# Turning attention's weights by DMA and VectorE instead of TensorE, with the second use of a pair two pairs later

## The chip, the cores and the metric

One core of a Trainium2 chip runs the whole program. The engines work side by side, each through its own instructions in order: TensorE (PE in the profile; PEld are its weight loads), VectorE (DVE), ScalarE (ACT), GpSimd (POOL) and SyncE (SP), which here only issues DMAs. The metric is device time in microseconds of one execution, as the median of several runs; the profile is of one execution.

## What is computed

The input is 2 images of 128 channels x 64 x 64. Layer 0 is a neighbourhood attention block per image. Layer 1 works on the 4096 tokens of each image: a full self-attention in which queries, keys and values are the same normalised tokens, and then a long-convolution mixer. The part that matters here:

```python
def _L1_attn_ref(q):
    scale = 1.0 / np.sqrt(HIDDEN_SIZE).astype(np.float32)
    sim = jnp.einsum('blh,bmh->blm', q, q) * scale
    diag = jnp.eye(L, dtype=bool)
    sim = jnp.where(diag[None, :, :], jnp.float32(-1000000000.0), sim)
    attn = jax.nn.softmax(sim, axis=-1)
    return jnp.einsum('blm,bmh->blh', attn, q)
...
t = _to_tokens(x)
t = t + _L1_attn_ref(_ln_t(t))
t = t + _L1_ffn_ref(_ln_t(t), ...)
```

All data are float32. `sim` is symmetric, so `exp(sim)` of a block of queries against a block of keys, turned, is the block of the keys against the queries. No maximum is subtracted, so the two halves need no rescaling.

## The kernel before

Stage 0 (to about 346 us) is layer 0, in an order written out by hand. Then come the attention of batch 0 (346 to about 790 us), the attention of batch 1 (to about 1266 us), and the convolution (the rest, from L1392 on). This change is in the attentions (lines 897 to 998).

The 4096 tokens of a batch are 8 chunks of 512. `cm[b]` holds them with channels on partitions (128 x 4096), `tok[b]` with tokens on partitions (32 tiles of 128 x 128). A pair (a, c) is a chunk a of queries against a chunk c >= a of keys: 28 pairs with a != c and 8 diagonal ones per batch, in the order of `pairs` (L910).

- `weights` (L913) makes one quarter k of a pair: a score matmul of 128 queries x 512 keys into a PSUM bank (L918), and ScalarE's exponential into an SBUF tile `e` (L926), which also sums the rows into `part`, the parts of the softmax denominators. On a diagonal pair only the columns from `lo` on are computed; VectorE adds a large negative number on the diagonal (L924), and the rest is filled from the quarters before by transposes (L932) and VectorE (L933).
- For a != c the four `e` are used twice. The first use (L983) multiplies `tok` of chunk a with each `e` and sums in the bank `other`: the output of chunk c. After four quarters VectorE adds it to `xa` (L995, or L997 for a = 0).
- The second use needs the weights turned. `turned` (L938) does this for 128 keys m: four TensorE transposes of 128x128 into a bank (L942), then one VectorE instruction that copies the bank to `et` and sums its rows into `part` (L945). `onto` (L952) multiplies `tok` of chunk c with `et` and sums in the bank `own`, the output of chunk a, over all c. When it is complete, VectorE adds it to `xa` (L960, L962) and `fill` is told.
- The loop (L969 to L998) makes the quarters of the following pair while it uses those of this one. The turned quarters wait in the list `late` and are used one by one behind the next products.
- After each quarter `fill()` does one step of other work: the rest of layer 0 (`drain`), the filter tables (`filters`, L1195; POOL writes `fb`, SP stores `gs` in L1222), the tokens of batch 1, and for each finished chunk `after` (L1003): layer norm, a transform on TensorE, `ub` on VectorE (L1039), and sixteen stores to `us` on SP's queue (L1043, L1048). In batch 1 it also loads and mixes the convolution's weights (`mixed`, L1166, with the loads `st` in L1171, two buffers).

Nothing in the attentions is in a hand-written order: a scheduler of the language places each engine's instructions from the order in which the program makes them, the dependences and its own estimates. Waits are on semaphores. All DMAs that SP issues go round eight completion counters: a DMA waits until the one eight before it has finished.

Of the kernel before, what the change touches and what calls it, by code (L numbers as in the profile page):

```python
# [8 lines left out]
F32 = mybir.dt.float32  # L9
AF = mybir.ActivationFunctionType  # L10
ALU = mybir.AluOpType
# [90 lines left out]
def kernel(  # L102
# [767 lines left out]
    with ap_:  # L870
        tp = ap_.enter_context(tc.tile_pool(name="l1_t", bufs=1, side="right"))
        ep = ap_.enter_context(tc.tile_pool(name="l1_e", bufs=8, side="right"))
        sp = ap_.enter_context(tc.tile_pool(name="l1_s", bufs=2, side="right"))
        ps_o = ap_.enter_context(tc.tile_pool(name="l1_ps_o", bufs=1, space=PSUM))
        ps_m = ap_.enter_context(tc.tile_pool(name="l1_ps_m", bufs=6, space=PSUM))
# [13 lines left out]
        one = tp.tile([P, 512], F32, name="one")  # L889
        nc.gpsimd.memset(one, 1.0)  # L890
# [6 lines left out]
        def attention(b, fill):  # L897
# [15 lines left out]
            def weights(a, c, k, left=()):  # L913
# [3 lines left out]
                ps = bank()  # L917
                nc.tensor.matmul(  # L918
                    ps[:, lo:], lhsT=cm[b][:, n * P : (n + 1) * P],
                    rhs=cm[b][:, CHUNKS[c] * 512 + lo : (CHUNKS[c] + 1) * 512], start=True, stop=True,  # L920
                )
                if a == c:
                    ks = slice(k * P, (k + 1) * P)
                    nc.vector.tensor_tensor(ps[:, ks], ps[:, ks], ndiag, ALU.add)  # L924
                e = ep.tile([P, 512], F32, tag="e", name="e")
# [3 lines left out]
                if lo:  # L929
                    pt = bank()  # L930
                    for j in range(k):
                        nc.tensor.transpose(pt[:, j * P : (j + 1) * P], left[j][:, lo : lo + P], ident)  # L932
                    nc.vector.tensor_tensor_reduce(  # L933
                        e[:, 0:lo], pt[:, 0:lo], one[:, 0:lo], 1.0, 0.0, ALU.mult, ALU.add, part[:, n, 8:9]
                    )
                return e

            def turned(a, c, m, es):  # L938

                pt = bank()  # L940
                for k in range(4):
                    nc.tensor.transpose(pt[:, k * P : (k + 1) * P], es[k][:, m * P : (m + 1) * P], ident)  # L942
                et = ep.tile([P, 512], F32, tag="et", name="et", bufs=4)
                n = 4 * CHUNKS[c] + m
                nc.vector.tensor_tensor_reduce(  # L945
                    et, pt, one, 1.0, 0.0, ALU.mult, ALU.add, part[:, n, a : a + 1]
                )
                return et

            own = None  # L950

            def onto(a, n, e, first, last):  # L952
                nonlocal own
                if first:
                    own = ps_o.tile([P, 512], F32, tag="own", name="own")
                nc.tensor.matmul(own, lhsT=tok[b][:, n, :], rhs=e, start=first, stop=last)  # L956
                if last:
                    xs = xa[b][:, chunk(a)]
                    if a:
                        nc.vector.tensor_tensor(xs, own, xs, ALU.add)  # L960
                    else:
                        nc.vector.tensor_copy(xs, own)  # L962
                    fill(CHUNKS[a], part)

            late = []
            es = []
            for k in range(4):
                es.append(weights(0, 0, k, es))
            for i, (a, c) in enumerate(pairs):  # L969
                following = pairs[i + 1] if i + 1 < len(pairs) else None  # L970
                coming = []
                if a != c:
                    other = ps_o.tile([P, 512], F32, tag="other", name="other")
                for k in range(0, 4, 2):
                    for j in (k, k + 1):
                        if following:
                            coming.append(weights(*following, j, coming))
                        if a == c:
                            while late:
                                onto(*late.pop(0))  # L980
                            onto(a, 4 * CHUNKS[a] + j, es[j], j == 0, a == 7 and j == 3)
# [740 lines left out]
```

## Time and profile before

| what | value |
|---|---|
| median of 3 runs | 2070.92 us (2066.39 to 2071.28) |
| the profiled execution: its own time, its span | 2070.7 us, 2068.7 us |
| TensorE busy over the span | 1997.5 us (97%) |
| VectorE, ScalarE, GpSimd busy | 997.7 (48%), 733.5 (35%), 472.9 us (23%) |
| granted TensorE clock, mean | 0.989 |
| data moved by DMA | 112.82 MB, 55 GB/s over the span |
| the chain that ended last | TensorE 80%, VectorE 7%, DMA 4%, GpSimd 4% |

The costliest groups of the attentions (line, engine, operation, tiles, shape, count, then busy us in all, mean ns of one, and the idle time just before them with what ended it):

```profile
L926 ACT ACTIVATE e<-bank 128x512 f32<-128x512 f32 (+3 forms) x288 | 161.6, 561 | 519.6 <-PE bank L918 396.5
L918 PE MATMUL bank<-cm 128*128 128x512 f32 (+3 forms) x576 | 277.4, 564 | 1.4 <-DVE y L664 1.4
L956 PE MATMUL own<-et,tok 128*128 128x512 f32 x448 | 230.2, 600 | 8.4 <-DVE part L945 8.1
L983 PE MATMUL other<-e,tok 128*128 128x512 f32 x448 | 229.9, 595 | 4.9 <-DVE xa L995 4.9
L945 DVE CUSTOM_DVE_ANT_0 et<-bank,one 128x512 f32<-128x512 f32 x224 | 146.1, 687 | 128.6 <-PE bank L942 128.4
L942 PE MATMUL bank<-ident,e 128*128 128x128 f32 x896 | 117.1, 274 | 0.0
```

Each float32 matmul is two instructions (448 for 224 products). Their durations overlap, so the mean is longer than what one adds to TensorE's time. ScalarE and VectorE stand idle before their instructions because they wait for TensorE; TensorE waits for next to nothing.

### The profile page before, as it was taken

The numbers are of one execution on the slowest core, as the hardware profiler recorded it, in microseconds if no ns is written. First come the engines' busy times: TensorE is split into PE (matmuls) and PEld (weight loads), VectorE is DVE, ScalarE is ACT, GpSimd is POOL, SyncE is SP. The second block draws the span as 40 slices with busy tenths as digits, with TensorE's granted clock in tenths as the row PEclk, the third lists the DMA queues.
The fourth block names the chain that finished last, engine by engine and source line by source line (L and its number), as shares of the span: only waits on it lengthen the run. The fifth ranks groups of instructions, "written<-read, shape, count | busy, mean of one in ns | idle before, by whom it ended". The sixth has DMA issues, their size and how long they took to land.

```text
span 2068.7 us, 52809 instructions
## 1 busy us (share of the span) xinstructions
PE 1997.5 (97%) x21368; PEld 1436.1 (69%) x21368; DVE 997.7 (48%) x3458; ACT 733.5 (35%) x1974; POOL 472.9 (23%) x781
## 2 busy tenths in 40 slices
PE   6899998999999999999999999999999999999998
PEld 4677775554555554554455554799999899999987
DVE  5899996444544445335733446333333333333332
ACT  3789885322322323212222322222222222222222
POOL 4466887215000000000000000022222121222211
PEclk8999999999999999999999999999999999999999
DMA  4222223003000001004200002222222123222211
GB/s 152 62 61 62 61 60 53 13 21 107 2 25 26 26 26 52 26 0 117 83 26 26 26 26 77 76 67 67 67 67 61 47 58 101 66 67 67 67 45 42
DMA packets 239506, 112.82 MB, mean 55 GB/s; under 512 B 118287, under 2 KB 237215, under 8 KB 238752
## 3 DMA queue, kind: packets, MB, share of 16 engines
q1 hardware_dynamic: 238338, 105.95, 18.9%
q8 instruction: 169, 2.77, 0.6%
q0 software_dynamic: 576, 2.10, 0.3%
q10 hardware_dynamic: 350, 1.41, 0.2%
q14 instruction: 73, 0.60, 0.1%
HBM read 74.78 MB, written 34.63 MB: 53 GB/s over the span
## 4 chain that ended last, share of the span: by engine, by line
PE 80%; DVE 7%; DMA 4%; POOL 4%; ACT 2%; SPq 2%; issue 1%; DVEq 0%; POOLq 0%; ACTq 0%
PE acc L1450 27%; PE own L956 11%; PE bank L918 9%; PE other L983 8%; PE pc L1431 7%; PE bank L942 4%; PE bank L343 2%; PE bank L201 1%; PE bank L1058 1%; PE bank L553 1%; DMA st<-in_m_minus_dram 1%; DMA st<-in_m_plus_dram 1%; ACT p L540 1%; PE bank L1101 1%; PE pc L1489 1%
## 5 line engine op out<-in xcount | busy, mean ns | idle before, releaser
L1436 DVE COPY y<-pc 128x512 f32<-128x512 f32 x320 | 206.2, 686 | 351.4 <-PE pc L1431 351.2
L926 ACT ACTIVATE e<-bank 128x512 f32<-128x512 f32 (+3 forms) x288 | 161.6, 561 | 519.6 <-PE bank L918 396.5
L1450 PE MATMUL acc<-y,mpl 32*128 32x256 f32 x5120 | 324.4, 380 | 0.8 <-DVE af L1460 0.8
L1450 PE MATMUL acc<-y,mmi 32*128 32x256 f32 x5120 | 316.7, 375 | 0.0
L1436 ACT COPY y<-pc 128x512 f32<-128x512 f32 x320 | 171.9, 589 | 400.9 <-PE pc L1431 396.1
L1450 PEld LDWEIGHTS acc<-y,mpl 32*128 32x128 f32 x5120 | 290.0, 186 | 8.2 <-DVE af L1460 1.8
L1450 PEld LDWEIGHTS acc<-y,mmi 32*128 32x128 f32 x5120 | 291.4, 185 | 3.8
L918 PE MATMUL bank<-cm 128*128 128x512 f32 (+3 forms) x576 | 277.4, 564 | 1.4 <-DVE y L664 1.4
L956 PE MATMUL own<-et,tok 128*128 128x512 f32 x448 | 230.2, 600 | 8.4 <-DVE part L945 8.1
L983 PE MATMUL other<-e,tok 128*128 128x512 f32 x448 | 229.9, 595 | 4.9 <-DVE xa L995 4.9
L1431 PE MATMUL pc<-ct,ut 32*128 32x256 f32 x2560 | 215.6, 382 | 5.6 <-DMA ut<-us 3.7
L945 DVE CUSTOM_DVE_ANT_0 et<-bank,one 128x512 f32<-128x512 f32 x224 | 146.1, 687 | 128.6 <-PE bank L942 128.4
L1461 POOL TENSOR_TENSOR af<-af 128x512 f32<-128x512 f32 x39 | 49.7, 1275 | 593.8 <-DVE af L1460 528.1
L173 POOL TENSOR_TENSOR ln_rs<-ln_rs,mhalf 128x4 f32<-128x4 f32 x24 | 24.2, 1009 | 703.6 <-DVE ln_rs L172 703.5
L1431 PEld LDWEIGHTS pc<-ct,ut 32*128 32x128 f32 x2560 | 175.7, 189 | 12.0 <-DMA ut<-us 4.5
L956 PEld LDWEIGHTS own<-et,tok 128*128 128x128 f32 x448 | 82.9, 190 | 121.8 <-issue 60.8
L983 PEld LDWEIGHTS other<-e,tok 128*128 128x128 f32 x448 | 81.7, 190 | 95.0 <-issue 86.9
L942 PEld LDWEIGHTS bank<-ident,e 128*128 128x128 f32 x896 | 103.0, 141 | 46.1 <-issue 39.4
L918 PEld LDWEIGHTS bank<-cm 128*128 128x128 f32 x576 | 94.5, 191 | 54.2 <-issue 38.9
L540 ACT ACTIVATE p<-p,mn 128x196 f32<-128x196 f32 x256 | 114.4, 449 | 13.7 <-DVE mn L530 13.0
L942 PE MATMUL bank<-ident,e 128*128 128x128 f32 x896 | 117.1, 274 | 0.0
L1039 DVE TENSOR_TENSOR ub<-bank,uo 128x256 f32<-128x256 f32 (+1 forms) x192 | 59.5, 373 | 71.1 <-ACT uo L1036 70.2
(258 smaller groups left out, 2530.8 us busy)
## 6 DMA issues: line engine op xcount, KB each, us to landing
ut<-us SPq DMA_DIRECT2D x160, 128.0 KB
us<-ub SPq DMA_DIRECT2D x128, 128.0 KB
ct<-gs SPq DMA_DIRECT2D x320, 40.0 KB
vw<-vd SPq DMA_DIRECT2D x256, 49.0 KB
ct<-gs SPq DMA_DIRECT2D x320, 32.0 KB
vd<-v SPq DMA_DIRECT2D x128, 32.0 KB
st<-in_m_plus_dram SPq DMA_DIRECT2D x16, 256.0 KB
us<-ub SPq DMA_DIRECT2D x128, 32.0 KB
```

Source lines behind the costliest of these rows:

```text
L540: nc.scalar.activation(p, p, AF.Exp, bias=t[name + "mn"][:, h : h + 1], scale=-1.0, accum_out=t["den"][:, u, h : h + 1],)
L918: nc.tensor.matmul(ps[:, lo:], lhsT=cm[b][:, n * P : (n + 1) * P], rhs=cm[b][:, CHUNKS[c] * 512 + lo : (CHUNKS[c] + 1) * 512], start=True, ...
L926: nc.scalar.activation(e[:, lo:], ps[:, lo:], AF.Exp, bias=0.0, scale=ASCALE, accum_out=part[:, n, c : c + 1])
L942: nc.tensor.transpose(pt[:, k * P : (k + 1) * P], es[k][:, m * P : (m + 1) * P], ident)
L945: nc.vector.tensor_tensor_reduce(et, pt, one, 1.0, 0.0, ALU.mult, ALU.add, part[:, n, a : a + 1])
L956: nc.tensor.matmul(own, lhsT=tok[b][:, n, :], rhs=e, start=first, stop=last)
L983: nc.tensor.matmul(other, lhsT=tok[b][:, 4 * CHUNKS[a] + j, :], rhs=es[j], start=(j == 0), stop=(j == 3))
L1039: nc.vector.tensor_tensor(ub[:, sgn, 0:n], pu[s][:, 0:n], half[:, 0:n], op)
L1431: nc.tensor.matmul(pcs[j].rearrange("p (g o c) -> p o g c", g=4, o=2)[:, :, at], lhsT=ut[rows_, par, :], rhs=cv_[rows_], start=True, stop= ...
L1436: (nc.scalar.copy if j % 2 else nc.vector.tensor_copy)(y[:, :, :, 4 * kl + j, :], pcs[j].rearrange("p (g x k) -> p k g x", g=4, k=KF))
L1450: nc.tensor.matmul(acc[j][:, 0:256], lhsT=(mmi if l else mpl)[rows_, k, :], rhs=y[rows_, k, 2 * l : 2 * l + 2].rearrange("p s n x -> p (s ...
L1461: eng.tensor_tensor(af[:, 0:2], af[:, 0:2], af[:, 2:4], ALU.add)
```

## The change

For pairs with a != c, the weights are turned without TensorE. A 128x512 quarter consists of 32x32 blocks; the turned matrix is the blocks moved to their mirrored places, and each block turned in itself.

- The four quarters of a pair lie in one tile of 128 x 2048. The score matmul reads the keys in the order (q, t, j) instead of (t, q, j), with key = 128 t + 32 q + j, so that what must go to one quarter of the partitions is contiguous.
- `moved` issues 16 DMAs on SP's queue. Each copies 32 partitions x 512 numbers from a quarter of the partitions of `e` to another (or the same) quarter of `et`.
- `turned` is now two VectorE transposes of 128x1024, which turn each 32x32 block in place, and one VectorE reduction over 2048 columns into `part` for four key tiles.
- The second use reads `et` in blocks of 32 columns and writes `own` in blocks of 32. It stands in the program four quarters after the transposes' place, which is itself four quarters after the DMAs: one pair (its first use) lies between the DMAs and the transposes, and the second use comes with the pair after that, two products after each of its first quarters. Two `own` banks are in use for this, and five banks instead of six for the rest.
- `other` comes out in the order (q, t, j) and is put back into (t, q, j) by the VectorE instruction that adds it to `xa`.
- On the diagonal pairs, the VectorE instruction that copied and summed at once becomes a copy and a reduction. The tile `one` and its fill go away.
- To make room, the filters' tables `ph` and `fsum` lie in `cm[1]`, which is empty then.

```diff
-        ep = ap_.enter_context(tc.tile_pool(name="l1_e", bufs=8, side="right"))
+        ep = ap_.enter_context(tc.tile_pool(name="l1_e", bufs=2, side="right"))
-        ps_m = ap_.enter_context(tc.tile_pool(name="l1_ps_m", bufs=6, space=PSUM))
+        ps_m = ap_.enter_context(tc.tile_pool(name="l1_ps_m", bufs=5, space=PSUM))
...
+                if k == 0:
+                    halves.append(ep.tile([P, 2048], F32, tag="e", name="e"))
+                eh = halves[0]
+                keys = cm[b][:, chunk(c)]
+                if a != c:
+                    nc.tensor.matmul(
+                        ps.rearrange("p (q t j) -> p q t j", q=4, t=4), lhsT=cm[b][:, n * P : (n + 1) * P],
+                        rhs=keys.rearrange("p (t q j) -> p q t j", t=4, q=4), start=True, stop=True,
+                    )
+                    e = eh.rearrange("p (q k r) -> p k q r", q=4, k=4)[:, k]
+                    nc.scalar.activation(
+                        e, ps.rearrange("p (q r) -> p q r", q=4), AF.Exp, bias=0.0, scale=ASCALE,
+                        accum_out=part[:, n, c : c + 1],
+                    )
+                    return e
...
-                    nc.vector.tensor_tensor_reduce(
-                        e[:, 0:lo], pt[:, 0:lo], one[:, 0:lo], 1.0, 0.0, ALU.mult, ALU.add, part[:, n, 8:9]
-                    )
+                    nc.vector.tensor_copy(e[:, 0:lo], pt[:, 0:lo])
+                    nc.vector.tensor_reduce(part[:, n, 8:9], e[:, 0:lo], AX.X, ALU.add)
...
-            def turned(a, c, m, es):
-
-                pt = bank()
-                for k in range(4):
-                    nc.tensor.transpose(pt[:, k * P : (k + 1) * P], es[k][:, m * P : (m + 1) * P], ident)
-                et = ep.tile([P, 512], F32, tag="et", name="et", bufs=4)
-                n = 4 * CHUNKS[c] + m
-                nc.vector.tensor_tensor_reduce(
-                    et, pt, one, 1.0, 0.0, ALU.mult, ALU.add, part[:, n, a : a + 1]
+            def moved(eh):
+
+                et = ep.tile([P, 4, 512], F32, tag="et", name="et", bufs=2)
+                for q in range(4):
+                    for to in range(4):
+                        nc.sync.dma_start(
+                            out=et[32 * to : 32 * to + 32, q], in_=eh[32 * q : 32 * q + 32, to * 512 : (to + 1) * 512]
+                        )
+                return et
+
+            def turned(et, a, c):
+
+                for q in (0, 2):
+                    flat = et[:, q : q + 2].rearrange("p q r -> p (q r)")
+                    nc.vector.transpose(flat, flat)
+                n0 = 4 * CHUNKS[c]
+                nc.vector.tensor_reduce(
+                    part[:, n0 : n0 + 4, a], et.rearrange("p q (k t i) -> p t (q k) i", k=4, t=4), AX.XY, ALU.add
                 )
...
+            def pair_onto(own, a, c, et, t):
+                onto(
+                    own, 4 * CHUNKS[c] + t, own.rearrange("p (k q i) -> p q k i", k=4, q=4),
+                    et.rearrange("p q (k t i) -> p t q k i", k=4, t=4)[:, t], False, c == 7 and t == 3,
+                )
+                if (c, t) == (7, 3):
+                    complete(a, own)
...
+                e = weights(a, c, k, left, halves)
+                if a != c and k == 3:
+                    et = moved(halves[0])
+                    turns.append((step + 4, et, a, c))
+                    late.extend((step + 5, a, c, et, t) for t in range(4))
+                return e
+
+            def pass_on(n):
+
+                while turns and turns[0][0] <= step:
+                    turned(*turns.pop(0)[1:])
+                while n and late and late[0][0] <= step:
+                    _, a, c, et, t = late.pop(0)
+                    pair_onto(owns[a], a, c, et, t)
+                    n -= 1
...
+                else:
+                    owns[a] = ps_o.tile([P, 512], F32, tag="own", name="own", bufs=2)
+                for j in range(4):
+                    if following:
+                        coming.append(coming_of(*following, j, coming, halves))
+                    n = 4 * CHUNKS[a] + j
+                    if a == c:
+                        onto(owns[a], n, owns[a], es[j], j == 0, a == 7 and j == 3)
+                    else:
+                        nc.tensor.matmul(
+                            other.rearrange("p (q r) -> p q r", q=4), lhsT=tok[b][:, n, :], rhs=es[j],
+                            start=(j == 0), stop=(j == 3),
+                        )
+                    pass_on(2)
+                    fill()
+                    step += 1
```

## The prediction

> **What bounds the kernel now.** I read first the busy time by window, for the two attentions (346 to 790 us is batch 0, 790 to 1266 batch 1), then the list of what TensorE waited for there, then its timeline over one pair of chunks.
>
> ```profile
> core 0: us, PE busy (x) PEld busy (x) DVE busy (x) ACT busy (x) POOL busy (x), PEclk, DMA share, GB/s
> 346.00:790.00 444.00, 436.87 (x1701) 230.13 (x1705) 204.15 (x750) 129.71 (x366) 73.61 (x83) 1.00 0.13 33
> 790.00:1266.00 476.00, 464.22 (x1755) 237.65 (x1749) 225.58 (x743) 120.98 (x357) 9.72 (x11) 1.00 0.14 42
> ```
>
> TensorE is busy for 901 of 920 us at full granted clock. VectorE is busy 47%, the DMA engines 14%: there is room to hand work to them. Some 19 us of TensorE waits are all that exists:
>
> ```profile
> PE own L956 <- DVE part L945: 8.1, 9, 1.6
> PE other L983 <- DVE xa L995: 4.9, 3, 2.5
> ```
>
> So time leaves only with TensorE work, and every new wait of TensorE is paid in full. The timeline of TensorE (start, duration) shows what a pair costs:
>
> ```profile
> 905.50 1.04 PE L942 MATMUL bank<-ident,e 128*128 128x128 f32 x8
> 906.38 1.02 PE L918 MATMUL bank<-cm 128*128 128x512 f32 x2
> 907.24 1.02 PE L983 MATMUL other<-e,tok 128*128 128x512 f32 x2
> 908.09 1.02 PE L956 MATMUL own<-et,tok 128*128 128x512 f32 x2
> ...
> 911.53 1.04 PE L942 MATMUL bank<-ident,e 128*128 128x128 f32 x8
> ```
>
> Starts count here, since durations overlap: a 512-wide float32 product (two instructions) takes 907.24 − 906.38 = 0.86 us, eight transposes 906.38 − 905.50 = 0.88 us. Half a pair is 911.53 − 905.50 = 6.03 us, which is 6 × 0.86 + 0.88. A pair is 12.06 us, of which 1.76 are transposes.
>
> **Removed.** All 896 transposes of L942, 112 groups of eight: 112 × 0.88 = 98.6 us. They lie on the path, since nothing is faster than TensorE there. This is the whole gain; the sum starts from the profiled execution's own 2070.7 us (span 2068.7, 2.0 around it), within 0.2 us of the median of the runs.
>
> **Kept on TensorE, in another shape.** Scores, `other` and the second use `own` keep count and width but read or write in runs of 32 elements. L1431 writes PSUM in permuted pieces at 382 ns, L1450 writes plainly at 380 for the same 256 columns: nothing. For the reads, the bound is the dearest row of the same 128x512 shape, L343 at 658 against 600 ns of L918: 0 to 58 ns on 56 × 12 = 672 products, 0 to 39 us. I take 0, because the nearest row is the permuted one.
>
> **VectorE.** Gone are four reductions with copy per pair, 4 × (0.687 + 0.083) = 3.08 us. New are two 32x32 transpositions of 128x1024 and one reduction of 2048.
>
> ```profile
> L1436 DVE COPY y<-pc 128x512 f32<-128x512 f32 x320 | 206.2, 686 | 351.4 <-PE pc L1431 351.2
> L1460 DVE COPY af<-acc 128x256 f32<-128x256 f32 x80 | 30.4, 420 | 97.8 <-PE acc L1450 95.1 <-ACT af L1460 2.7
> L1461 POOL TENSOR_TENSOR af<-af 128x512 f32<-128x512 f32 x39 | 49.7, 1275 | 593.8 <-DVE af L1460 528.1
> ```
>
> From the two copies: (686 − 420) / 256 = 1.04 ns a column and 154 ns fixed; 1024 columns 1.22 us, 2048 columns 2.28 us. No row is a transposition. Its bounds are 0.96 us (twice the fastest 512-wide VectorE row, L1174 at 481) and 2.55 us (twice GpSimd's 1.275). I take 1.22, the engine's own rate. VectorE then gives 4.72 us per pair instead of 3.08, 56 × 1.64 = 92 us more, some 60% busy in the attentions (430 + 92 of 863 us); that is hidden beside TensorE as long as nothing TensorE needs stands behind it. What does: in the built order of the changed program the usual row on VectorE is first transposition, eviction of `other` (0.69 us), second transposition, reduction. The eviction is ready at the end of a pair, so the second transposition ends 0.8 + 1.22 = 2.02 us into the next pair, where TensorE has a score and an `other` product, 1.72 us, ahead of the second use. Late by 0.3 us: 56 × 0.3 = 17 us. With 0.96 it would be 2, with 2.55 it would be 56 × 1.63 = 91. The 48 diagonal rests (L933) become a copy and a reduction; a copy is no longer than what it replaces and the reduction (0.3 to 0.55 us) is wanted only by the later denominator: 0, at most 5.
>
> The Trainium skill, page "VectorE: DVE Perf Modes", section "The three transpose paths", speaks against the edit: it lists 390 ns for TensorE and 311 ns for VectorE's blocks at 128x128 in bf16, and its rules give the full transposition to TensorE. Eight times 311 would be an estimate of 2.5 us per 128x1024, and the sum 2085 us; no row here shows it, while the copies' slope is 1.04 ns a column.
>
> **The moves.** 56 × 16 = 896 DMAs of 32 partitions x 2 KB (64 KB) are added on SP's queue, 1 MB a pair.
>
> ```profile
> 0.82 1.82 SPq L135 DMA_DIRECT2D xa<-in_x_dram  x4
> 40.28 17.21 SPq L504 DMA_DIRECT2D vw<-vd  x22
> 567.76 4.96 SPq L1043 DMA_DIRECT2D us<-ub  x8
> 574.84 4.51 SPq L1048 DMA_DIRECT2D us<-ub  x8
> ```
>
> SP hands out a DMA every 1.82 / 4 = 0.455 us where each row is one run in one partition (as the moves are), every 17.21 / 22 = 0.78 where partition is an inner dimension. I take 0.455: 7.3 us a pair. From issue to the last completion count, the trace's records have 1.9 us (median of us<-ub, 128 KB) to 2.9 us (st, 256 KB); I take 2.1. Packets: 1 KB takes 46 ns and 4 KB 159 in the records, so some 85 for 2 KB, 512 × 0.085 / 16 = 2.7 us a pair of the sixteen engines. Not a limit.
>
> Is it in time? From the end of a pair's last score to its second use TensorE has an `other` (0.86), four scores and four `other` (6.9), four uses of the pair before (3.4) and a score (0.86): 12.0 us, and the other work between. That is 920 less 56 × 12.06, less 16 × 6.25 (a diagonal, by its products), less 19 idle, over 72 pairs: 1.8. So 13.8 us, and a pair lasts 10.3 + 1.8 = 12.1. Needed: exponential and handover 0.9, 15 issues 6.8, landing 2.1, second transposition 1.3: 11.1. Slack 2.7 us.
>
> SP's other work now queues with the moves, and VectorE's transposition behind them, and TensorE behind that. The stores of `us` (4.96 + 4.51 us a chunk, 16 chunks) hold SP for 4.7 of a pair's 12.1 us, so they meet the moves about four times in ten, with a mean delay of half that, 2.4 us, mostly inside the slack: I take 10 us, bounds 0 and 16 × (9.5 − 2.7) = 109. The 32 loads `st` in batch 1 (L1171) make SP wait 44 us in all for a buffer; before nobody stood behind them, now about five pairs of moves do. I take a third, 15 us, bounds 0 and 44.
>
> The page "DMA: Bandwidth & Descriptors" of the Trainium skill, section "Bandwidth", gives 0.95 us of engine span for 64 KB and calls less than that mostly overhead. Sixteen in a row would be an estimate of 15.2 us against a pair of 12.1, 56 × 3.1 = 174 lost and a sum near 2146 us; the us<-ub rows, 128 KB every 0.62 us with 1.9 to land, show transfers overlapping instead.
>
> Buffers: two tiles of 2048 columns replace eight e of 512, two replace four et, `own` has two banks and the bank ring five instead of six. A tile e is wanted again 0.9 us after its pair's end; its `other` products end with the pair and its moves 3 us earlier (7.3 + 2.1 against 12.1). A pair draws four banks where it drew eight. The filters' tables now lie in the still empty `cm` of batch 1, whose first eviction by ScalarE comes after the filters' last read in program order. Nothing for these three; if a cover fails, it is a fraction of a microsecond a pair, inside A's range. The dropped fill of `one` on GpSimd, once, is nothing.
>
> **Sum.** 2070.7 − 98.6 + 17 + 10 + 15 = 2014 us.
>
> **Rivals.** A, the above: 2014, own range 1975 to 2045, chance 0.55.
>
> B, SP's queue becomes the bound, the slower side. Place: SP in both attentions. SP's other work is 76 us of `us` stores and half of 86 for the rest (32 st at 0.42 and their 44 us of waits, 32 gs and 16 ct at 0.6) per attention, 119. At 0.78 us a move it is 448 × 0.782 + 119 = 469 us, against 460 that an attention takes today: 2 × 9.5 = 19 more than today, and the 17 of VectorE behind it, 2107. It binds from (411 − 119) / 448 = 0.65 us a move (411 being the attention without transposes) and is slower than before from 0.76. For: most rows of SP are at 0.6 to 0.78, and each move waits for the move eight earlier. Against: those rows have the partition inside, and eight moves at 0.455 are 3.6 us, longer than a landing. Chance 0.20.
>
> C, VectorE's queue becomes the wait: the reduction stands ahead of the eviction, or a transposition costs near 2.55. The first costs 2.28 − 0.86 = 1.4 us a pair where the order is so; in half the pairs 40 us, total 2037 with the 25 of SP. The second gives 91 in place of 17: 2088; break-even is a transposition of 2.2 us. For: 60% busy and strictly in order. Against: the built order mostly has the eviction first. Middle 2060, chance 0.17.
>
> D, reads in runs of 32 slow TensorE: 2014 + 39 = 2053. For: no row shows such a read at this width. Against: L1431. Chance 0.08.
>
> **How the numbers follow.** About 0.3% (6 us) is what can be told from no change. A is all faster (0.55); C gives 0.08 faster, 0.03 same, 0.06 slower; D 0.04, 0.02, 0.02; B 0.01 same, 0.19 slower. Faster 0.67, same 0.06, slower 0.27. The time is A's, 2014. From 1975 (A without any new wait is 1972) to 2100 about half of B and a little of A stay out, 0.13.
>
> **What will show it.** Right: the attentions together near 865 us, no L942, moves issued every 0.4 to 0.5 us, a transposition of 1.1 to 1.4 us, TensorE waiting for et some 0.3 us a pair. Wrong: moves at 0.6 us or more with SP never idle (B); a transposition above 2 us or `other` waiting for its eviction a microsecond a pair (C); scores starting more than 0.86 us apart back to back (D).

## The result and the profile after

The change is slower. The kernel after takes 2127.57 us (median of 4 runs, 2123.65 to 2133.09) against 2070.7 of the kernel before beside it; the ratio is 1.0281, with an interval of 1.0254 to 1.0308. The forecast was 2014, its range ended at 2100. The profiled execution has a span of 2126.0 us (before 2068.7).

The first view is the busy time by window of the kernel after, in the same two windows and the same columns as before (PE, PEld, DVE, ACT, POOL, then granted clock and DMA share):

```profile
346.00:790.00 444.00, 392.00 (x1199) 178.75 (x1200) 252.93 (x575) 119.69 (x351) 71.89 (x81) 0.97 0.38 94
790.00:1266.00 476.00, 405.03 (x1187) 180.44 (x1186) 268.30 (x539) 110.27 (x336) 8.71 (x10) 0.95 0.37 98
```

TensorE was busy 901 of these 920 us before and is busy 797 now, although the attentions are not finished at 1266: their last product on TensorE now ends at about 1316. So TensorE idles, in work that has lost 98.6 us of products. The clock column tells a second loss: it was 1.00 in both windows and is 0.97 and 0.95. The same 448 instructions of the second use have a mean of 630 ns where they had 600.

The second view is the list of groups of the kernel after (busy time and mean ns of one, then the idle time before it and what ended it):

```profile
L969 PE MATMUL own<-et,tok 128*128 128x512 f32 x448 | 217.8, 630 | 26.0 <-DVE et L962 18.6
...
L962 DVE STREAM_TRANSPOSE et<-et 128x1024 f32<-128x1024 f32 x112 | 138.9, 1240 | 111.8 <-DMA et<-e 102.2
...
L964 DVE TENSOR_REDUCE part<-et 128x4 f32<-128x2048 f32 x56 | 127.6, 2279 | 0.9
```

The new VectorE instructions cost what was forecast (1240 ns against 1220, 2279 against 2280). What is new is the idle time in front of the transposition: 102 us of VectorE standing still for the moves.

The third view is the list of waits of the kernel after from 340 to 1260 us (who waited for whom: total, times, longest):

```profile
ACT e L926 <- DMA et<-e: 118.4, 16, 19.0
DVE et L962 <- DMA et<-e: 97.4, 38, 6.6
...
ACT e L937 <- DMA et<-e: 65.6, 8, 14.3
...
PE other L1025 <- ACT e L926: 42.6, 14, 12.2
...
PE bank L943 <- ACT e L937: 27.2, 8, 7.4
...
PE own L969 <- DVE et L962: 15.1, 15, 2.4
```

Read from below: TensorE waits for ScalarE's exponential more than for the turned tile. ScalarE waits for a tile `e`, of which there are two, and a tile is free when its moves have landed. That is the cover that the prediction put at nothing.

The last two views are timelines of the kernel after over the same stretch, SP first (start, duration of the group, instructions), then VectorE (in brackets the idle time before and what ended it):

```profile
1068.37 10.10 SPq L953 DMA_DIRECT2D et<-e  x16
1078.57 6.25 SPq L1089 DMA_DIRECT2D us<-ub  x8
1084.91 10.02 SPq L953 DMA_DIRECT2D et<-e  x16
1095.03 4.58 SPq L1094 DMA_DIRECT2D us<-ub  x8
1099.72 1.84 SPq L953 DMA_DIRECT2D et<-e  x3
```

```profile
1091.48 1.25 DVE L962 STREAM_TRANSPOSE et<-et 128x1024 f32<-128x1024 f32 x1 [6.04 <-DMA et<-e]
1095.27 0.69 DVE L1036 TENSOR_TENSOR xa<-other,xa 128x512 f32<-128x512 f32 x1 [2.54 <-PE other L1025]
1096.54 1.25 DVE L962 STREAM_TRANSPOSE et<-et 128x1024 f32<-128x1024 f32 x1 [0.58 <-DMA et<-e]
```

SP has no gap from 1068 to 1101: sixteen moves take 10.0 to 10.1 us, which is 0.63 us each, and the stores of `us` put 6.25 and 4.58 us between two pairs' moves. And VectorE has the eviction of `other` between the two transpositions of one pair, and stands idle for the moves before both. Two suspects, then: SP's queue, and the order in which the instructions were built. The experiments had to part them, and for a while they did not.

### The profile page after: what moved, and what is told of

Same layout as the page of the kernel before. It is cut to its first block, busy times and chain, and to the rows that moved or that the text cites. A ratio compares the mean times of both kernels' runs of the same rounds, so it can differ in the third digit from the quotient of the medians.

```text
span 2126.0 us, 52422 instructions
## 1 busy us (share of the span) xinstructions
PE 1941.1 (91%) x20472; PEld 1348.2 (63%) x20472; DVE 1126.8 (53%) x3178; ACT 723.5 (34%) x1974; POOL 472.2 (22%) x780
## 4 chain that ended last, share of the span: by engine, by line
PE 61%; SPq 14%; DVE 9%; DMA 6%; POOL 4%; issue 3%; ACT 2%; DVEq 0%; ACTq 0%; POOLq 0%
PE acc L1497 26%; SPq L953 12%; PE own L969 7%; PE pc L1478 7%; PE bank L921 4%; PE other L1025 3%; PE bank L343 2%; DMA et<-e 2%; DVE et L962 2%; PE bank L553 2%; PE bank L201 1%; DMA us<-ub 1%; SPq L1094 1%; PE bank L517 1%; PE bank L1147 1%
## 5 line engine op out<-in xcount | busy, mean ns | idle before, releaser
L926 ACT ACTIVATE e<-bank 128x512 f32<-128x512 f32 x224 | 132.6, 596 | 403.0 <-PE bank L921 222.2
L969 PE MATMUL own<-et,tok 128*128 128x512 f32 x448 | 217.8, 630 | 26.0 <-DVE et L962 18.6
L921 PE MATMUL bank<-cm 128*128 128x512 f32 x448 | 232.3, 609 | 0.7 <-ACT tt L219 0.7
L962 DVE STREAM_TRANSPOSE et<-et 128x1024 f32<-128x1024 f32 x112 | 138.9, 1240 | 111.8 <-DMA et<-e 102.2
L969 PEld LDWEIGHTS own<-et,tok 128*128 128x128 f32 x448 | 88.9, 203 | 146.8 <-issue 99.1
L964 DVE TENSOR_REDUCE part<-et 128x4 f32<-128x2048 f32 x56 | 127.6, 2279 | 0.9
L921 PEld LDWEIGHTS bank<-cm 128*128 128x128 f32 x448 | 77.8, 193 | 70.9 <-issue 51.5
L937 ACT ACTIVATE e<-bank 128x512 f32<-128x512 f32 (+1 forms) x64 | 27.9, 438 | 180.0 <-DVE bank L935 100.9
```

The source lines that it names most:

```text
L921: nc.tensor.matmul(ps.rearrange("p (q t j) -> p q t j", q=4, t=4), lhsT=cm[b][:, n * P : (n + 1) * P], rhs=keys.rearrange("p (t q j) -> p ...
L926: nc.scalar.activation(e, ps.rearrange("p (q r) -> p q r", q=4), AF.Exp, bias=0.0, scale=ASCALE, accum_out=part[:, n, c : c + 1],)
L962: nc.vector.transpose(flat, flat)
L964: nc.vector.tensor_reduce(part[:, n0 : n0 + 4, a], et.rearrange("p q (k t i) -> p t (q k) i", k=4, t=4), AX.XY, ALU.add)
L969: nc.tensor.matmul(out_, lhsT=tok[b][:, n, :], rhs=e, start=first, stop=last, skip_group_check=True)
```

## The experiments

Each time stands beside that of the kernel before on the same chip (2067.4 to 2070.7 us). Where no interval is given, the time is of one execution; differences of some 5 us are not read then. The theory at the start was S: the issue of 16 transfers on SP.

**How many issues? 4 and 8 instead of 16.**

```diff
+                for q in range(4):
+                    nc.sync.dma_start(out=et[:, q], in_=eh[:, q * 512 : (q + 1) * 512])
```

> Leaves out the change of partition quarter: each pair's weights go to the second tile by 4 transfers of 128 partitions x 2 KB instead of 16 of 32 partitions x 2 KB, so the same 1 MB a pair, the same 512 packets of 2 KB, the same lag, transpositions and products; only the number of issues falls. Theory S (SP's issue of 16 transfers a pair, some 0.635 us each, 10.2 us of a pair's 12, fills SP's queue; the tile e is then released late, ScalarE and TensorE wait): the moves take SP under 2.5 us a pair, the attentions lose the stalls on the exponential (L926) and the TensorE clock goes back above 0.985; 1985 to 2030 us. Rival W (the bytes: 1 MB a pair is too much beside the other traffic): nothing changes, 2100 us or more. Rival V (VectorE's transpositions and reduction ahead of the evictions): nothing changes, 2100 us or more. Rival R (TensorE's reads in runs of 32): score and own products still slower, 2060 or more with no waits on the exponential.

Measured: 1998.6 us.

```diff
+                for q in range(4):
+                    for h in (0, 64):
+                        nc.sync.dma_start(out=et[h : h + 64, q], in_=eh[h : h + 64, q * 512 : (q + 1) * 512])
```

> Leaves out the change of partition quarter, like the straight copies, but with 8 transfers of 64 partitions x 2 KB a pair, on SP alone: between the 4 issues that gave 1998.6 us and the 16 of the change (2127.6). Theory S (issues on SP): 8 x 0.635 = 5.1 us a pair on SP, done 5 us before the second use needs it; what is lost is lost around SP's other work only: 2005 to 2035 us. If the time went with the size of the pieces (64 or 32 partitions against 128) and not with the count on one queue, about half of the loss: 2060 or more.

Measured: 1990.3 us, the best time of the study (without the change of quarter). Here is its busy time by window:

```profile
346.00:790.00 444.00, 430.54 (x1399) 202.57 (x1398) 291.82 (x701) 140.51 (x402) 77.90 (x87) 0.99 0.44 106
790.00:1266.00 476.00, 459.11 (x2022) 230.43 (x2024) 301.89 (x625) 130.84 (x369) 13.32 (x20) 0.98 0.43 113
```

TensorE is back at 890 of 920 us, and the attentions' last product ends at about 1181 us (1265 before, 1316 in the change), so these windows hold part of the convolution too. The DMA engines are busier than in the change (0.44 against 0.38), the 2 KB packets as slow (median 147 ns against 141; 84 in the run with 4 transfers), and the kernel is 137 us faster than the change. So bytes and packets (W), VectorE's work (V) and TensorE's reads in runs of 32 (R), all of which are the same here, are out as causes of the loss.

**Crossing the quarters, or the shape of the pieces?**

```diff
-                            out=et[32 * to : 32 * to + 32, q], in_=eh[32 * q : 32 * q + 32, to * 512 : (to + 1) * 512]
+                            out=et[32 * to : 32 * to + 32, q], in_=eh[32 * to : 32 * to + 32, q * 512 : (q + 1) * 512]
```

> Leaves out the change of partition quarter: 16 transfers of 32 partitions x 2 KB a pair on SP as in the change, but each within its own quarter. Theory S (count of issues on SP): nothing changes against the change itself, 2110 to 2140 us. If the crossing between quarters were what is slow: 1985 to 2040 us.

Measured: 2130.5 us, the time of the change (the difference of 3 us is not read). Crossing quarters is not what costs.

```diff
+                for h in range(2):
+                    for q in range(4):
+                        to = (q + 1 + h) % 4
+                        nc.sync.dma_start(
+                            out=et[32 * to : 32 * to + 32, 2 * h : 2 * h + 2].rearrange("p q r -> p (q r)"),
+                            in_=eh[32 * q : 32 * q + 32, h * 1024 : (h + 1) * 1024],
+                        )
```

> 8 transfers a pair on SP that do cross the quarters, 32 partitions x 4 KB each, the same 1 MB; the places within the quarters are not those of the change, so the weights land in wrong order. Theory S (count): 5.1 us a pair on SP, 1985 to 2035 us. If crossing quarters or pieces of only 32 partitions were what is slow: 2060 us or more.

Measured: 2085.5 us, a miss for theory S, and the run that turned the study. The number lies where the rival had it, but the rows below speak against pieces of 32 partitions as its reason. The two rows are from the view of the tile `et`, first of this kernel, then of the one with 8 transfers of 64 partitions (issue time in ns, least, median, most):

```profile
L954 SPq DMA_DIRECT2D et<-e x448: 507/589/2021, 365.3 to 1258.6; - x150
```

```profile
L953 SPq DMA_DIRECT2D et<-e x448: 461/595/1877, 365.0 to 1166.3; - x150
```

The issue costs the same, and so does the landing (medians 2.34 and 2.36 us). SP has the same work, and yet one is 95 us slower. What differs is the built order. In the built programs I counted, for each pair of chunks, the products of the attention on TensorE between its fourth score and its second use, and in how many of the 56 pairs the four second uses stand in one block:

| kernel | in one block | products between | us |
|---|---|---|---|
| 4 transfers | 1 | 13.7 | 1998.6 |
| 8 of 64 partitions | 9 | 14.1 | 1990.3 |
| 8 of 32 partitions | 54 | 20.1 | 2085.5 |
| 16 (the change, and within a quarter) | 54 | 20.1 | 2127.6, 2130.5 |

On VectorE, with 8 of 64 partitions both transpositions of a pair stand ahead of the eviction of its own `other` in 46 pairs. In the change, in none: one stands behind it in 17 pairs, both in 18, and in 21 pairs the second stands behind the eviction of the next pair. TensorE, VectorE and ScalarE have the same instructions; the scheduler places them by its own estimates, and the shape of the moves is all that it sees differ. That it counts pieces of 32 partitions as late is inferred from that, not shown.

**Less on SP, or more room, with the order as it came.** These five were made before the order was seen, and in all of them it came out much as in the change: 49 to 55 pairs in one block, 19.7 to 27.7 products between.

```diff
-                            nc.sync.dma_start(
+                            nc.scalar.dma_start(
                                 out=to[:, ri], in_=ub[:, sgn, :].rearrange("p (f d) -> p f d", d=P)
```

(and the same at L1094)

> The moves stay as they are; the stores of us (L1089, L1094), 9.5 us of SP a chunk, go to ScalarE's queue. Theory S: SP in a row of pairs has 10.2 us of moves and about 1.5 of other work a 12.1 us pair instead of 10.2 and 4; it still has little room, but the backlog grows only around the loads and gs stores: 2040 to 2090 us. Rival W, V, R: no change, 2120 to 2135. If only the latency of the 16 moves mattered and not SP's other work, also no change.

Measured: 2115.4 us, a miss. A view of its waits shows a new one:

```profile
SPq L953 <- DMA us<-ub: 95.0, 64, 28.8
```

A move waits until the DMA eight earlier has finished, and the eight completion counters are shared by SP's and ScalarE's queues: the moves now wait for stores of another queue.

```diff
-                            nc.sync.dma_start(
+                            nc.gpsimd.dma_start(
```

(at L1089, L1094, L1217 and L1269)

> The 16 moves of a pair stay on SP; the stores of us (L1089, L1094), the loads st (L1217) and the stores of gs (L1269) go to GpSimd's queue, which has its own completion counters, so SP has in both attentions little but moves. It divides the loss in two. Part Q (moves standing behind SP's other work and its waits for buffers) goes; part L (16 issues of 0.635 us last 10.0 us, so that a pair needs 0.9 + 9.5 + 2.0 + 1.3 = 13.7 us of the 13.5 it has, and the next pair's moves begin late) stays. Clean rows of the change lose some 3 to 8 us each against the straight copies, 14 rows: 40 to 70 us of part L, so 2040 to 2075 us. If L were all, 2115 to 2130; if Q were all, 2000 to 2015.

Measured: 2094.9 us: only 33 us went, and more stayed than the expectation gave to part L.

```diff
-                    turns.append((step + 4, et, a, c))
-                    late.extend((step + 5, a, c, et, t) for t in range(4))
+                    turns.append((step + 5, et, a, c))
+                    late.extend((step + 6, a, c, et, t) for t in range(4))
```

> The change with transposition and second use one step (a quarter of a pair, some 3 us) later; the moves are issued where they were and the tiles e are released when they were. If TensorE and VectorE waiting for the turned tile is what costs (the budget of 13.8 us too short by 1 to 3 us a pair): 2060 to 2095 us. If the release of the two tiles e by the moves, and behind it ScalarE's exponential, is what costs: 2110 to 2130 us, since it is not touched.

Measured: 2106.1 us, between the two ranges: it decides neither.

```diff
-        ep = ap_.enter_context(tc.tile_pool(name="l1_e", bufs=2, side="right"))
+        ep = ap_.enter_context(tc.tile_pool(name="l1_e", bufs=3, side="right"))
```

> The change with three tiles e instead of two; the room comes from the copies of ub, fb and fn (4 to 2), uo (2 to 1) and z4 (2 to 1), which may cost something of its own. If the release of e is what costs, ScalarE runs one pair further ahead of a late queue: 2060 to 2095 us. If SP simply has no room in a row of pairs, TensorE waits for the turned tile instead of for the exponential: 2110 to 2135 us.

Measured: 2143.6 us. ScalarE's waits for the moves become shorter (340 to 1330 us: 118.4 to 20.8 us at L926, 67.5 to 34.4 at L937), TensorE's for the turned tile longer (`own` 45.4 us, where the change has 18.6). The wait moves on and nothing is won; what the copies given up for it cost can't be parted from that here.

```diff
+                wd = dram.tile([P, 2048], F32, tag="wd", name="wd", bufs=4)
+                nc.sync.dma_start(out=wd, in_=eh)
+                for to in range(4):
+                    nc.sync.dma_start(
+                        out=et[32 * to : 32 * to + 32],
+                        in_=wd.rearrange("(q x) c -> x q c", q=4)[:, :, to * 512 : (to + 1) * 512],
+                    )
```

> The full result by another way: a pair's weights are written to a buffer in DRAM by one transfer of 128 partitions x 8 KB and read back into the partition quarters by 4 transfers of 32 partitions x 4 x 2 KB, so 5 issues a pair instead of 16, twice the bytes, two trips one after the other (2.0 us each by the landing of the moves, perhaps 3). Theory S: SP spends 2 to 4 us a pair, the data is there some 6 to 8 us after the last exponential instead of 12, the stalls on the exponential go; 1985 to 2040 us, faster than the kernel before. Rival W (bytes): 2 MB a pair makes it worse than the 2128 of the change. Rival V or R: 2060 or more.

Measured: 2192.4 us, ratio 1.0603 [1.058, 1.0626], a miss for theory S and, in its number, what W had. But the order differs too. Two trips of 5.0 and 5.7 us (medians from issue to landing) instead of one of 2.0, and the built order with the second use farthest behind (27.7 products). What the detour would cost in another order was not tried.

**The complete change, with the moves on two queues.**

```diff
-                        nc.sync.dma_start(
+                        (nc.sync, nc.scalar)[to % 2].dma_start(
```

> The 16 moves of a pair as they are, every other one issued by ScalarE's queue instead of SP's: 5.1 us a pair on each. Theory S: SP has 5 us a pair of room again, moves are all issued some 5 to 6 us after the last exponential; ScalarE, busy 30%, issues 5 us a pair more, and its next exponential may stand behind a move; 2010 to 2070 us. Rival W (bytes), V, R: nothing changes on the engine that limits, 2100 or more.

Measured: 2033.4 us, ratio 0.9822 [0.9803, 0.9841]. With the second use a step later:

> The moves split between SP and ScalarE (2033 us) and the second use one step later. If what the split still loses against the 8 transfers on SP alone (1990 us) is a turned tile that is late after collisions: 2005 to 2025 us. If it is ScalarE held by its own moves' waits: 2028 to 2040 us.

Measured: 2033.5 us; the later use brings nothing, as expected if ScalarE's own moves hold it up; that it is these is not shown. With GpSimd in ScalarE's place (`nc.gpsimd`):

> The change complete, every other move issued by GpSimd instead of SP: 8 issues of 0.635 us on SP, 8 on GpSimd, which is nearly idle in the attentions and stands before no exponential. GpSimd's four loads in the trace of before (L795, 512 KB each) took 5.4 to 7.6 us to land against 2.0 us of SP's moves; so a pair needs at most 0.9 + 5 + 6.5 + 1.3 = 13.7 us of its 13.5 to 13.8. Theory S: 1990 to 2050 us, faster than before and than the split with ScalarE (2033) if GpSimd's small transfers land in 2 to 4 us. If the landing is 6 us or more: 2050 to 2100 us.

Measured: 2018.1 us, ratio 0.9766 [0.974, 0.9792]: the complete result, 51 us faster than before. GpSimd's moves landed after 2.73 us (median), not after 6.5. In all three the order came out as in the fast ones (4 to 8 in one block, 14.0 to 14.9 products). So these runs, too, changed both suspects, the load of SP and the order, at once.

**The order alone: first try.** The attention's products are held on TensorE in the order in which the program makes them:

```diff
-                    nc.tensor.matmul(
+                    tc.keep_in_program_order(nc.tensor.matmul(
```

(scores, diagonal scores, `other`, `own`)

> The change complete, all 16 moves on SP, only that the attention's products (scores, diagonal scores, other, own) are held on TensorE in the order in which the program makes them. In the built order of the change the four second uses of a pair stand in one block in 54 of 56 pairs, on average 20.1 products of the attention behind the pair's fourth score; in the eight versions with this order (2085 to 2192 us) alike, in the four others (1990 to 2033 us) it is 14. With the order held it is 10 of 56 and 14.8. Theory O (the built order is what costs; the issues on SP only led the scheduler to it): 1995 to 2060 us. Theory S (16 issues of 0.635 us on SP are what costs): 2110 to 2135 us, or more, since the second use now stands earlier.

Measured: 2153.0 us, ratio 1.0417 [1.0399, 1.0434].

> The 8 crossing transfers of 32 partitions x 4 KB (2085 us, weights in wrong places as there), with the products held in the order of the program. SP's queue had room in that run, and the pieces landed in 2.3 us. Theory O: 1985 to 2020 us, beside the 1990 of the 8 transfers of 64 partitions. If pieces of 32 partitions cost something on the chip: unchanged, 2075 to 2095 us.

Measured: 2075.8 us.

> The change complete, moves split between SP and GpSimd (2018 us), with the products held in the order of the program. Its built order has 8 of 56 pairs in one block, all but one in two rows of batch 1. Theory O: those rows lose their stalls, 1990 to 2012 us. If the 28 us over the 8 transfers on SP alone (1990) come from GpSimd's slower landings: 2012 to 2025 us.

Measured: 2056.6 us, ratio 0.9944 [0.9924, 0.9963]. Three misses for the order as I stated it. The third is the control: a kernel whose order was good lost 39 us by the holding (from the second use of a row's last pair to that of the next row's first, across the diagonal, it took 24.7 to 26.5 us in most rows, where the same split had 21.7 without the holding), and VectorE's order was left to the scheduler. In the first two runs only 3 of 56 pairs have both transpositions ahead of the eviction of their own `other` (46 in the fast version with 8 transfers), and in the second TensorE still waits 55.5 us for the transposition (`own`): TensorE's order alone is not the order. The hold was too crude to settle anything.

**The order alone: second try, two by two.** TensorE, VectorE and ScalarE have the same instructions, in the same order of the program, in the change and in the version with 8 transfers of 64 partitions. So the built order of either can be given to the other, all three engines at once, by an edge from each instruction to the one before it. SP and GpSimd keep what the scheduler gives them:

```diff
+        for before, now in zip(places, places[1:]):
+            tc.add_manual_dep(traced[engine][now], traced[engine][before].name, free, reason="order")
...
     with tile.TileContext(nc) as tc:
         tile_hybrid_kernel(tc, *args)
+        _hold(tc)
```

> The 8 transfers of 64 partitions (1990.3 us), with every instruction of TensorE, VectorE and ScalarE held in the order that the scheduler built for the change. The three engines have the same instructions in both programs, only the order differs. Theory O (the built order costs by itself, whatever the moves cost): 2070 to 2100 us, as the 8 transfers of 32 partitions had in that same order (2085.5). If the order is harmless and the moves decide: 1985 to 2005 us.

> The reverse: the change complete, 16 moves on SP, with TensorE, VectorE and ScalarE held in the order that the scheduler built for the 8 transfers of 64 partitions. If the order is the only cause: 1990 to 2030 us. If SP's queue (10 us of moves a pair, and the stores of us, 4.6 us at a time, ahead of them) costs on the chip by itself: a row with stores goes at 14.7 us a pair as in the order held as written, against 10.6; 2070 to 2130 us. Something between says how much each does alone.

| us | order built for the 8 transfers | order built for the change |
|---|---|---|
| 8 transfers of 64 partitions | 1990.3 | 2080.0 |
| 16 moves | 2159.7 | 2127.6 |

In the traces, VectorE and ScalarE run instruction by instruction in the order that they were given, and TensorE has the same counts of pairs in one block and products between. So the table parts the two. The order costs 90 us by itself, with 8 transfers that the fast version hides. Sixteen moves in place of 8 cost 169 us by themselves, in the order that the fast version has. Together they cost 137, less than the moves alone: in the order of the change the turned tile is used later, and VectorE waits 97.4 us for moves where it waits 236.7 in the other order (340 to 1260 us). Three of the four times are of one execution each, but the differences are far beyond 5 us. That the edges themselves cost the 90 is unlikely: the 8 pieces of 32 partitions, without any edge, had nearly this order and took 2085.5.

This fits the earlier runs, without being tested on them: the loads and stores on GpSimd (2094.9) and the 8 pieces of 32 partitions (2085.5) are near the 2080 that the order leaves once SP has room, and the 16 moves with TensorE's products held (2153.0) are near the 2160 that SP leaves once TensorE's order is short.

How the order costs is seen on VectorE with the 8 transfers in the order of the change. For one pair the last move was issued at 1058.6 us, and landings take 2.4:

```profile
1070.44 0.69 DVE L1034 TENSOR_TENSOR xa<-other,xa 128x512 f32<-128x512 f32 x1 [9.31 <-PE other L1023]
1071.05 1.23 DVE L960 STREAM_TRANSPOSE et<-et 128x1024 f32<-128x1024 f32 x1
```

Everything for this second transposition had landed by about 1061, but it stands behind an eviction that waits for TensorE to end the next pair. It runs 10 us later, and the second use of the pair right behind it, at 1072.3. Here TensorE comes just then and does not wait. In the whole run it waits 51.8 us for the transposition (`own`, 346 to 1266 us), 21 times. Eight of the waits are of 1.4 us, a transposition behind the next pair's eviction. The four longest, 28 us together, come between 970 and 1034 us, where VectorE's order has the mixing of the convolution's weights (L1220 and its neighbours, which wait for the loads `st`) ahead of the transpositions. The longest of them, for a pair whose moves had landed by 990.2 us (three lines of VectorE, then TensorE):

```profile
1001.65 1.24 DVE L960 STREAM_TRANSPOSE et<-et 128x1024 f32<-128x1024 f32 x1
1007.97 0.75 DVE L1220 SCALAR_TENSOR_TENSOR mmi<-st,wt,mmi 128x512 f32<-128x512 f32 x1 [2.16 <-DMA st<-in_m_minus_dram]
1011.78 1.24 DVE L960 STREAM_TRANSPOSE et<-et 128x1024 f32<-128x1024 f32 x1
1013.07 3.78 PE L967 MATMUL own<-et,tok 128*128 128x512 f32 x4 [9.87 <-DVE et L960]
```

How the moves cost by themselves is seen in the waits of the 16 moves in the order built for the 8 transfers, from 340 to 1260 us:

```profile
DVE et L962 <- DMA et<-e: 236.7, 70, 9.0
...
PE other L1025 <- DVE xa L1036: 40.4, 16, 7.8
PE own L969 <- DVE et L962: 37.0, 17, 5.4
```

VectorE stands for the moves with the transposition, and with it everything queued behind: the eviction of `other`, for which TensorE waits.

The last run gave that order to the best complete version:

> The change complete with its moves split between SP and GpSimd (2018 us), in the order built for the 8 transfers of 64 partitions. Its own built order differs from that one in few places of TensorE, so it should stay within 2000 to 2025 us; below 2005 if the few places are what it loses against 1990, above 2015 if GpSimd's landings are.

Measured: 2031.0 us, ratio 0.9818 [0.9802, 0.9834], slower than the 2018.1 in its own order, and outside what was expected. So the 28 us between the split and the 8 transfers on SP are not explained by these few places; what they are stays open.

This run says one thing more. Beside the 2159.7 it has the same 16 moves and the same order of TensorE, VectorE and ScalarE; only the queue that issues half of the moves differs. That takes away 129 of the 169 us. So most of what the sixteen moves cost lies in their going through one queue, not in their number or size on the way. The other 41 us (2031.0 against 1990.3) stay open. So do the 13 us by which this run is slower than the split in its own order: they may be a cost of the edges, and the 169 can hold some of the same. The split between SP and GpSimd in its own order is the version that beats both kernels.

## Why the prediction was wrong

**Removed, 98.6 us: right as far as the runs can show it.** With 8 transfers the kernel gains 80.4 of them (2070.7 − 1990.3), with all of the change in place but the change of quarter.

**TensorE's reads in runs of 32, 0 of 0 to 39 us: right.** The second use has a mean of 593 ns with 8 transfers, 600 before. Rival D falls.

**VectorE: the sizes right, the place wrong.** 1.24 and 2.28 us a piece, as forecast. But "late by 0.3 us" was worked out for one row (transposition, eviction, second transposition) taken as usual, with the eviction at the end of the pair. It holds so in 17 of 56 pairs; in 21 the eviction ahead of the second transposition is the next pair's, a whole pair later.

**The budget of 13.8 us: wrong, this is the first failed step; the order costs 90 us.** It counted 14 products between the last score and the second use, from the loop as written. The built order has 20.1. The prediction read VectorE's built order (and generalised one row of it) and took TensorE's from the source. The same table that shows 20.1 would have shown that the second use stands in one block behind a whole further pair, and that the tiles, two of each, are held that much longer.

**The moves: landing right, issue wrong, this is the second failed step and the larger.** 2.02 us against 2.1 to land. (The 2 KB packets took 141 ns and not 85, as the fast version's did with 147; nothing was lost by it that the runs show.) The issue takes 0.589 us plus 0.045 to the next, 0.63 against the 0.455 taken from `xa<-in_x_dram`; the row with "one run in one partition" was the wrong likeness, and the prediction itself names most rows of SP as 0.6 to 0.78. Sixteen are 10.1 us, not 7.3, and the prediction's own sum is then 0.9 + 9.5 + 2.0 + 1.3 = 13.7 of 13.8: no slack for the stores, whose delay it had put "mostly inside the slack". In place of 10 + 15 us for these collisions, sixteen moves cost 169 by themselves, and 129 of these go when half of the issues leave SP. This step alone is enough for the miss: in the run of 2159.7 us the budget is as forecast, 14.1 products between, and the time is 146 over the forecast. The first step alone gives 2080.0.

**Rival B: the right place, the wrong test.** It said that SP binds from 0.65 us a move, by the sum of an attention, and that the kernel is slower than before from 0.76; at 0.63 neither should have come. SP's issue durations add up to 324 of the 444 us of the first window, 73%. The sum hides that a diagonal has no moves, while a row (the pairs of one chunk a) has them without a pause: between 1068 and 1101 us SP has no gap, and what it is behind there it can't make up by idling at the diagonal. Its outcome (slower, SP never idle) came, at a price below its threshold.

**Buffers, nothing: wrong, but not shown to be a cause of its own.** ScalarE waits 118.4 + 65.6 us for the tile `e`. A third one did not help: TensorE then waited for the turned tile instead, though that run gave up other copies for it.

**Rival C** had VectorE's queue as the wait, by its work: a dear transposition, or the reduction ahead of the eviction. The queue was the wait, but by its order, with the durations as forecast. The Trainium skill, "VectorE: DVE Perf Modes", section "The three transpose paths", lists 311 ns for VectorE's blocks at 128x128 in bf16. The estimate of 2.5 us per 128x1024, eight times that, is not borne out for this float32 shape: 1.24 us.

**The other page.** The Trainium skill, "DMA: Bandwidth & Descriptors", section "Bandwidth", gives 0.95 us for 64 KB, measured from HBM to SBUF with GpSimd issuing; these moves go from SBUF to SBUF. The estimate made of it, a sum near 2146, came close to the time, but not for its reason: with 8 transfers of 128 KB the DMA engines were busier than in the change (0.44 against 0.38) and the kernel took 1990.3 us.

## What to carry to other kernels

Where a scheduler places instructions, a transfer changes the program twice: once on the chip, by its issue, and once in the built order of every engine, since the scheduler places instructions by its own estimates. So count a latency budget in the built order, engine by engine, with whatever else stands in it (here the mixing of weights for a later stage), and where an experiment changes a transfer's shape, compare the built orders before reading its time as a price of the transfer. A queue that is busy three quarters on average can be the bound of every stretch that matters: work out its load over a row of the loop, with what lies between, not over the stage.

## What the runs showed of the hardware

- The issue of a transfer between two tiles of SBUF on SP took 0.59 to 0.60 us for all four shapes that were run: 32, 64 or 128 partitions x 2 KB (0.589, 0.595, 0.600), 32 x 4 KB (0.589). To DRAM with 128 x 8 KB it was 0.350, back from it with 32 x 4 x 2 KB 0.428.
- GpSimd issued the same moves at 0.496 us, and they landed in 2.73 us (on SP 2.02); its only rows in the trace before, 512 KB each, had 5.4 to 7.6.
- Where TensorE idled more, its granted clock was lower. In the two attention windows it was 1.00 and 1.00 before (busy 901 of 920 us), 0.99 and 0.98 with 8 transfers (890), 0.97 and 0.95 in the change (797). Over the whole run it was 0.989, 0.986 and 0.971, and 0.964 for 16 moves in the other order.
